# A graph layer with linear attention and an expert FFN: gates from features not yet normed, the list of other slots behind the first gathers, a slot's result by halves in one step, and its last rows gathered sooner

## The chip, the cores and the metric

The kernel runs on one core of a Trainium2 chip. The metric is the device time of one execution in microseconds (us), as the median of several runs. A core has five engines with an instruction stream each: TensorE (PE, matrix products; its weight loads are shown apart as PEld), VectorE (DVE), ScalarE (ACT), GpSimd (POOL) and SyncE (SP). In this kernel SP issues the ordinary DMAs, and POOL issues the indirect ones, which gather or scatter rows by a list of row numbers. Matrix results land in PSUM, a memory of eight banks; everything else is in SBUF, 128 partitions wide.

## The reference

There are 1250 nodes with 768 features. Three sublayers follow one another; the first two add to the same input.

```python
xn = layernorm(x)
x  = x + gnn(xn) + mix(xn)          # gnn: two graph attention layers, then concat([xn, out2]) @ Wu + bu
x  = x + ffn(layernorm(x))          # mix: linear attention with 12 heads, then @ Wo + bo

def ffn(xt):                        # 8 experts, 768 -> 384 -> 768
    gate = xt @ Wg + bg
    scores, idx = top_k(gate, 2)
    h = gelu(einsum('td,edh->eth', xt, W1) + b1)
    y = einsum('eth,ehd->etd', h, W2) + b2
    comb = sum(one_hot(idx, 8) * scores[..., None], axis=1)
    return einsum('te,etd->td', comb, y)
```

`layernorm` has no gain and no bias: it takes off the mean of a row and divides by its standard deviation. `out2` is the output of the second graph layer, 2 heads of 96 features. The gate's scores are used as they are, without a softmax. Everything is float32.

## The kernel before, in words

*Stages.* Up to about 620 us the kernel norms x and computes the two graph attention layers and the sums of the linear attention. What the graph layers leave is `o2T`, the second layer's output per head, turned, and `rd2`, one over its softmax sums. Then two stages follow that the change touches.

*The pair stage* (some 620 to 885 us). The nodes are 10 tiles of 125 rows, taken as 5 pairs. The loop `for p in range(NT // 2)` computes for both tiles of a pair x + mix + gnn. It first loads the two tiles of x (`xt`, L932) and adds the biases `bu_b` to them (L933). Then it calls `query(p + 1)`, the query products of the next pair, and then makes the present pair's products with `Wu` and `Wo`. The products with `Wq` and `Wu` are by quarters: a pair of tiles is a 2 x 2 array of blocks, and seven products of sums and differences of blocks replace eight. Each is a sequence of matmuls into one PSUM bank (`product`, L801), which VectorE then adds into the query or into xt (`add`, L945). `s_p` is the pool of 4 such banks, and `mm_p` the pool for turning and for other products. After the even tile's last product comes `finish(2 * p, ...)`, after the odd tile's `finish(2 * p + 1, ...)`.

*finish(t, xt)* (L853 to L922) does the rest for one tile, in this order. Four products of `o2T` with the last rows of Wu (L860) are the graph part; VectorE scales each by `rd2` and adds it to xt (L862). xt goes to the output (L865). `normalise` (L300 to L311) makes the normed row `xl` from it: statistics (L307, L308), standard deviation on ACT (L309), reciprocal (L310), result (L311). xl goes to `xl_d` in DRAM (L870). `turn` (L314 to L321) transposes xl by six TensorE transposes, three to a bank, and ACT copies each bank (L321). Six matmuls with `Wg` give the gates (L875, two records each), VectorE adds the bias (L878), and the 8 gates are written to `xl_d` beside the row (L880). VectorE ranks the 8 gates of each node (L887 to L896); `sel` marks its two experts. A product with a triangle of ones and one with `ones` and the running count `cum` (L900) give each node's place within its experts; adding `base` (L903) makes it a place in the whole list. An expert has NJ = 10 slots of 128 rows. The place is cut into slot and row within the slot by integer steps (L909 to L914), both become one-hot matrices (`hot` L918, `put` L920), and their product (L922) adds node numbers into `inv`, the PSUM tile of row lists, 128 rows by 80 slots.

*Between the stages* (L977 to L1012). After the last tile VectorE turns `inv` into `idx`, the row lists in SBUF (empty places point to a spare row). SP issues the loads of experts 1 to 3 (`expert`, L692 to L700: W1, W2 and the bias `wb` spread over the partitions). Then VectorE works out the list of other slots: the first FIX = 3 slots of each expert are always computed, the others only where nodes fill them. That is a chain of small VectorE operations on tiles of 8 to 64 elements, with three small TensorE steps, which ends in `v_row` and `e_row` (number and expert of the other slots in order) and `n_more` (how many there are). Here there is one.

*The expert stage* (some 903 us to the end). For each expert, `gather` (L1021) fetches its three slots: POOL issues an indirect DMA of 128 rows of 776 numbers (L1027), TensorE turns them by six transposes into `px` (L1030), VectorE copies px in two halves (L1033) into `xsT` and copies the gate column (L1036). px is one PSUM buffer of two banks (`x_p`, bufs 1). `inner` (L1039) makes `ph` = W1 times xsT for 384 rows (L1046) and ACT makes gelu of it, `hT` (L1048). The next expert's gather is called here, ahead of `give`. `give` (L1051) makes `py` for each slot (L1058), VectorE adds the bias row `wb` to all 768 columns in one step (L1061), ACT multiplies by the gate (L1062), and POOL issues an indirect DMA that adds the rows `ys` into the output (L1063). Two buffers each serve py and ys. Then the weights of expert e + 4 are called for (four weight buffers). After the loop `other(0)` does the same for the first other slot: it reads its number and expert into registers (L1082, L1084), copies its rows and bias, loads its expert, gathers, computes and scatters. `others(1)` does the rest under an If, and has nothing to do here.

*What sets the order.* The program is written as one sequence, and the framework spreads it over the engines. Each engine runs its own instructions in a fixed order in which priorities decide and which isn't wholly that of the text; between engines semaphores make an instruction wait for its inputs, and for the last use of a buffer that it overwrites. An instruction that waits holds up all behind it on its engine. DMAs share 8 semaphores in turn, so an SP or POOL instruction may also wait for an earlier DMA on the same semaphore.

## Time and profile before

| | |
|---|---|
| median of 3 runs | 1147.31 us (1145.44 to 1149.77) |
| the profiled execution, its own time | 1146.65 us |
| its span, first to last instruction | 1144.8 us |
| mean granted TensorE clock | 0.976 |
| PE, PEld | 1046.8, 700.9 us busy (91%, 61%) |
| DVE, ACT, POOL | 705.8, 347.9, 74.2 us busy (62%, 30%, 6%) |
| DMA | 79.76 MB, mean 70 GB/s |

Busy time by stretch of the profiled execution:

| stretch, us | PE | DVE | ACT | POOL | granted clock |
|---|---|---|---|---|---|
| 0 to 400 | 350.83 | 304.50 | 158.83 | 7.23 | 0.99 |
| 400 to 620 | 205.65 | 165.91 | 109.21 | 2.97 | 0.98 |
| 620 to 885 (pairs) | 264.32 | 171.96 | 39.02 | 0.00 | 1.00 |
| 885 to 915 (between) | 12.94 | 14.69 | 1.14 | 5.51 | 0.61 |
| 915 to 1112 (experts) | 197.00 | 44.91 | 35.78 | 52.28 | 0.99 |
| 1112 to 1145 (end) | 16.09 | 3.80 | 3.91 | 6.21 | 0.79 |

How to read such rows: a row of the timeline begins with the start and the busy length in us, then engine, line of the code, operation, output and inputs by the program's names, shapes, and how many instructions are joined in the row; in brackets stand the idle time before it and what ended it. A group of instructions on PE that overlap is given by its whole length. The clock is the share of full speed that TensorE was granted. The span leaves out what lies before the first and after the last instruction; the execution's own time has it.

### The profile page before, as it was taken

The numbers are of one execution on the slowest core, as the hardware profiler recorded it, in microseconds if no ns is written. First come the engines' busy times: TensorE is split into PE (matmuls) and PEld (weight loads), VectorE is DVE, ScalarE is ACT, GpSimd is POOL, SyncE is SP. The second block draws the span as 40 slices with busy tenths as digits, with TensorE's granted clock in tenths as the row PEclk, the third lists the DMA queues.
The fourth block names the chain that finished last, engine by engine and source line by source line (L and its number), as shares of the span: only waits on it lengthen the run. The fifth ranks groups of instructions, "written<-read, shape, count | busy, mean of one in ns | idle before, by whom it ended". The sixth has DMA issues, their size and how long they took to land.

```text
span 1144.8 us, 12035 instructions
## 1 busy us (share of the span) xinstructions
PE 1046.8 (91%) x4482; PEld 700.9 (61%) x4482; DVE 705.8 (62%) x1439; ACT 347.9 (30%) x522; POOL 74.2 (6%) x98
## 2 busy tenths in 40 slices
PE   2699998999999989988999999999999499999994
PEld 2596655579696969544554556666665256666653
DVE  7866767569696967769685857566665422222210
ACT  2141114464655555174743211120200011111121
POOL 1000000000000000000000000000000212223221
PEclk9999999999999999989999999999999599999997
DMA  5015000000000000200035011112045638787543
GB/s 161 28 31 189 14 28 1 1 1 1 1 1 1 1 1 3 80 1 1 14 129 169 12 41 41 47 36 63 20 158 180 197 72 220 208 215 189 118 63 50
DMA packets 35542, 79.76 MB, mean 70 GB/s; under 512 B 7006, under 2 KB 15536, under 8 KB 35468
## 3 DMA queue, kind: packets, MB, share of 16 engines
q1 hardware_dynamic: 29868, 59.06, 16.0%
q0 software_dynamic: 5600, 19.77, 8.6%
q8 instruction: 39, 0.64, 0.2%
q14 instruction: 35, 0.29, 0.1%
HBM read 60.48 MB, written 18.34 MB: 69 GB/s over the span
## 4 chain that ended last, share of the span: by engine, by line
PE 67%; DVE 23%; DMA 3%; issue 2%; ACT 2%; SPq 0%; POOL 0%; DVEq 0%; POOLq 0%; ACTq 0%
PE s L801 16%; PE ph L1046 9%; PE mm L599 8%; PE py L1058 7%; PE mm L430 7%; DVE scr L520 6%; DVE w L540 5%; DVE w L541 5%; PE ag L553 3%; PE mm L860 2%; PE ag L575 2%; PE mm L405 2%; PE px L1030 2%; PE ec L350 1%; PE g L875 1%
## 5 line engine op out<-in xcount | busy, mean ns | idle before, releaser
L553 PE MATMUL ag<-kept,w 125*125 125x198 f32 x800 | 137.5, 333 | 5.1 <-DVE w L541 4.8
L553 PEld LDWEIGHTS ag<-kept,w 125*125 125x125 f32 x800 | 133.5, 188 | 9.0 <-DVE w L541 9.0
L1046 PE MATMUL ph<-xsT,w 128*128 128x384 f32 (+1 forms) x324 | 102.3, 478 | 2.7 <-DVE xsT L1033 2.7
L1058 PE MATMUL py<-w,hT 128*128 128x384 f32 x300 | 100.6, 486 | 0.0
L430 PE MATMUL mm<-Wg,xnT 128*125 128x400 f32 x240 | 90.1, 513 | 1.1 <-DVE xnT L321 0.6
L540 DVE TENSOR_TENSOR w<-v,w 125x1250 f32<-125x1250 f32 x60 | 86.4, 1456 | 6.6 <-ACT w L538 5.9
L599 PE MATMUL mm<-Wv_sb,xnT 128*125 128x384 f32 x240 | 85.8, 490 | 4.8 <-DVE kvacc L619 4.8
L520 DVE CUSTOM_DVE_ANT_0 scr<-ss_row,mask 125x1250 bf16<-125x1250 f32 x60 | 87.4, 1456 | 0.5 <-ACT ss_row L511 0.2
L1046 PEld LDWEIGHTS ph<-xsT,w 128*128 128x128 f32 x324 | 61.5, 201 | 42.2 <-DVE xsT L1033 3.4
L541 DVE SCALAR_TENSOR_TENSOR w<-w,AT 125x1250 f32<-125x1250 f32 x60 | 86.5, 1457 | 0.4
L539 ACT ACTIVATE v<-dn_row,sl 125x1250 f32<-125x1250 f32 x60 | 79.3, 1333 | 17.0 <-DVE w L540 16.5
L599 PE MATMUL mm<-Wk_sb,xnT 128*125 128x384 f32 x240 | 84.5, 486 | 0.0
L801 PE MATMUL s<-w,qT 128*125 128x384 f32 x240 | 83.7, 491 | 0.0
L1033 DVE COPY xsT<-px 128x384 f32<-128x384 f32 x50 | 25.5, 552 | 87.3 <-PE px L1030 87.3
L1058 PEld LDWEIGHTS py<-w,hT 128*128 128x128 f32 x300 | 55.4, 190 | 33.8
L1061 DVE TENSOR_TENSOR ys<-py,wb 128x768 f32<-128x768 f32 x25 | 23.9, 958 | 74.1 <-PE py L1058 50.8
L599 PEld LDWEIGHTS mm<-Wv_sb,xnT 128*125 128x125 f32 x240 | 42.5, 187 | 31.1 <-DVE kvacc L619 6.9
L801 PEld LDWEIGHTS s<-w,qT 128*125 128x125 f32 x240 | 43.3, 188 | 26.9 <-issue 0.2
L538 ACT ACTIVATE w<-up_row,s 125x1250 f32<-125x1250 f32 x40 | 53.3, 1331 | 17.8 <-PE ag L553 17.6
L430 PEld LDWEIGHTS mm<-Wg,xnT 128*125 128x125 f32 x240 | 42.6, 190 | 26.1 <-ACT v L367 1.3
L599 PEld LDWEIGHTS mm<-Wk_sb,xnT 128*125 128x125 f32 x240 | 42.2, 187 | 23.5 <-issue 1.7
L356 DVE TENSOR_TENSOR AT<-AT,ec 125x120 f32 x162 | 44.4, 274 | 19.8 <-PE ec L350 18.6
(296 smaller groups left out, 1466.9 us busy)
## 6 DMA issues: line engine op xcount, KB each, us to landing
w<-in_L_ffn_W_dram SPq DMA_DIRECT2D x18, 1152.0 KB
xt<-in_x_dram SPq DMA_DIRECT2D x20, 336.0 KB
wb<-in_L_ffn_b_dram SPq DMA_DIRECT2D x9, 384.0 KB
out_dram<-xt SPq DMA_DIRECT2D x10, 336.0 KB
xl_d<-xl SPq DMA_DIRECT2D x10, 336.0 KB
W_sb<-in_L_gnn_W_dram SPq DMA_DIRECT2D x1, 2304.0 KB
Wk_sb<-in_L_mix_Wk_dram SPq DMA_DIRECT2D x1, 2304.0 KB
Wv_sb<-in_L_mix_Wv_dram SPq DMA_DIRECT2D x1, 2304.0 KB
```

The source lines that it names most:

```text
L356: nc.vector.tensor_add(here, here, ec[:, g])
L430: nc.tensor.matmul(ps[:PT, :2 * (CG + 2)], xnT[:, c, t * PT:(t + 1) * PT], Wg1[:, c, 2 * k:2 * k + 2].rearrange("p h c -> p (h c)"), start ...
L520: nc.vector.tensor_tensor_reduce(scr, ss_row, mask[:, t], 1.0, 0.0, ALU.mult, ALU.max, top[:, t:t + 1])
L538: nc.scalar.activation(w, up_row, AF.Exp, bias=ss[:, st:st + 1])
L539: nc.scalar.activation(v, dn_row, AF.Exp, bias=sl[:, st:st + 1])
L540: nc.vector.tensor_tensor(w, v, w, op=ALU.max)
L541: nc.vector.scalar_tensor_tensor(w, w, 2.0, AT[:, st, :N], op0=ALU.min, op1=ALU.mult)
L553: nc.tensor.matmul(ag[:, t // 2, o:o + CG], w[:, t * PT:(t + 1) * PT], gw[:, st, hd], start=st == 0 and t % 2 == 0, stop=st == NT - 1, ski ...
L599: nc.tensor.matmul(ps[:PT, :384], xnT[:, c, t * PT:(t + 1) * PT], w[:, c, half], start=c == 0, stop=c == KC - 1)
L801: nc.tensor.matmul(ps, left[:, c], right[:, c], start=start and c == 0, stop=c == n - 1, skip_group_check=True)
L1046: nc.tensor.matmul(ph[:, :n * 128], w[0][:, o:o + 128], xT[:, c, :n * 128], start=c == 0, stop=c == KC - 1)
L1058: nc.tensor.matmul(py[:, k, :384], hT[:, f, j * 128:(j + 1) * 128], w[:, o:o + 384], start=f == 0, stop=f == FC - 1)
```

## The change

The tile's graph part is taken out of `finish` into `second(t, xt)`, which the pair loop calls for each tile as soon as its x and biases are in xt, ahead of `query(p + 1)`. In `finish` the transposes and the gate product take xt, not the normed xl. Since xl = (xt - mean) / sd, the gates follow as (xt Wg - mean times the column sums of Wg) / sd + bg: `Wg_s`, the column sums, is made once by a product of ones with Wg, and VectorE needs `nrs` (minus one over sd), `off` and the gate step in place of one addition. The part `base` of a node's place comes from a third product into pp, so the addition `at` goes; `slot_row` counts in steps of 128, so the slot needs no shift: `row_f` is the place's last seven bits, `slot_f` the rest.

Between the stages, only `total` is still computed ahead of the gathers. The rest of the list stands behind the first `gather`, with its constants in the longer-lived pool `fp`, and its transposes go into the pool of ph.

`gather` issues all its DMAs ahead of the transposes, and px is now a half with a bank of its own (`x_p`, bufs 2). In `give`, py is a half of 384 columns in one bank (`y_p`, bufs 4); ACT multiplies the bias row by the gate ahead of it (`gb`), and VectorE makes ys from PSUM in one step per half, py times gate plus gb. The other slot's register loads, rows, bias and weights (`other`) come at the end of the loop's step e = 4, where the ring has no more to load, and its gather comes with the call for expert 7, ahead of expert 7's py products; the rest of it (`run`) stays behind the loop.

The line numbers after the change, where they differ: products L813, graph part L872 and L874, gates L891, `off` L896, gate L898, places L920, `row_f` L932, `slot_f` L933, hot and put L937 and L939, inv L941, xt's load and biases L951 and L952, `total` L997 and L999, `idx` L1001 and L1002, gather L1018, px L1027, xsT L1028, gates' column L1031, ph L1041, hT L1043, gb L1050, py L1057, ys L1059, scatter L1061, register loads L1069 and L1071, list L1096 to L1120.

The diff, cut to its core:

```diff
+        Wg_s = rp.tile([PT, NE], F32)
+        all1 = rp.tile([128, PT], F32)
+        nc.gpsimd.memset(all1, 1.0)
+        pf = g_p.tile([128, 2 * NV], F32, name="g")
+        for c in range(KC):
+            nc.tensor.matmul(pf[:PT, :NE], all1, Wg_sb[:, c], start=c == 0, stop=c == KC - 1)
+        nc.scalar.copy(Wg_s, pf[:PT, :NE])
...
-        def finish(t, xt):
+        def second(t, xt):
             tk = tokens(t)
             for h in range(H2):
...
                     nc.vector.scalar_tensor_tensor(xt[:, half], ps[:PT, :384], rd2[:, h, t:t + 1],
                                                    xt[:, half], op0=ALU.mult, op1=ALU.add)
+
+        def finish(t, xt):
...
-            normalise(xl[:, :D], xt)
+            mv, rs = normalise(xl[:, :D], xt)
+            nrs = rl.tile([PT, 1], F32, name="nrs")
+            nc.vector.tensor_scalar(nrs, rs, -1.0, None, op0=ALU.mult)
...
-            turn(xT, xl, mm_p, "mm", nc.scalar.copy)
+            turn(xT, xt, mm_p, "mm", nc.scalar.copy)
...
-            nc.vector.tensor_add(gate, pg[:PT, :NE], bg_b)
+            nc.vector.scalar_tensor_tensor(off, Wg_s, mv[:, 0:1], pg[:PT, :NE], op0=ALU.mult,
+                                           op1=ALU.subtract)
+            nc.vector.scalar_tensor_tensor(gate, off, nrs, bg_b, op0=ALU.mult, op1=ALU.add)
...
-            for i, (l, r) in enumerate(((tri, sel), (ones, cum[:, t]))):
+            for i, (l, r) in enumerate(((ones, base), (ones, cum[:, t]), (tri, sel))):
...
-            at = rl.tile([PT, NE], F32, name="at")
-            nc.vector.tensor_add(at, pp[:PT, :NE], base)
...
-            nc.vector.tensor_single_scalar(s_i[:, 0], b_i, 7, op=ALU.arith_shift_right)
-            nc.vector.tensor_single_scalar(s_i[:, 1], b_i, 127, op=ALU.bitwise_and)
-            s_f = rl.tile([PT, 2, 2], F32, name="s_f")
-            nc.vector.tensor_copy(s_f, s_i)
+            nc.vector.tensor_single_scalar(r_i, b_i, 127, op=ALU.bitwise_and)
+            nc.vector.tensor_copy(row_f, r_i)
+            nc.vector.tensor_sub(slot_f, both, row_f)
...
                 nc.vector.tensor_add(xt, xt, bu_b)
+                second(t, xt)
                 x2.append(xt)
...
+        pt = g_p.tile([128, 2 * NV], F32, name="g")
+        nc.tensor.matmul(pt[:, :NE], ones, cum[:, NT], start=True, stop=True)
+        total = fp.tile([128, NE], F32)
+        nc.vector.tensor_copy(total, pt[:, :NE])
         free = rp.tile([128, NV], F32)
...
-        more = rp.tile([128, NE, NJ - FIX], F32)
...
-            nc.vector.tensor_scalar(row, pr[:1, :128], add, None, op0=ALU.add)
...
-    x_p = ctx.enter_context(tc.tile_pool(name="x_p", bufs=1, space=PSUM))
+    x_p = ctx.enter_context(tc.tile_pool(name="x_p", bufs=2, space=PSUM))
...
-    y_p = ctx.enter_context(tc.tile_pool(name="y_p", bufs=2, space=PSUM))
+    y_p = ctx.enter_context(tc.tile_pool(name="y_p", bufs=4, space=PSUM))
...
+        got = []
+        for r in rows:
+            xg = sp.tile([128, D + NE], F32, name="xg", bufs=3)
+            nc.gpsimd.indirect_dma_start(xg, None, xl_d, bass.IndirectOffsetOnAxis(r, 0))
+            got.append(xg)
...
+        for j, xg in enumerate(got):
             for a in range(2):
+                px = x_p.tile([128, 512], F32, name="px")
+                for c in range(3):
+                    o = (3 * a + c) * 128
+                    nc.tensor.transpose(px[:, c * 128:(c + 1) * 128], xg[:, o:o + 128], ident)
                 nc.vector.tensor_copy(xT[:, 3 * a:3 * a + 3, j * 128:(j + 1) * 128],
-                                      px[:, a, :384].rearrange("p (b n) -> p b n", b=3))
+                                      px[:, :384].rearrange("p (b n) -> p b n", b=3))
...
+        gb = sp.tile([128, D], F32, name="gb")
+        nc.scalar.mul(gb, wb, gates)
+        ys = sp.tile([128, D], F32, name="ys")
+        for k in range(2):
+            half = slice(k * 384, (k + 1) * 384)
+            py = y_p.tile([128, 512], F32, name="py")
+            for f in range(FC):
                 o = KC * FF + f * D + k * 384
...
-        nc.vector.tensor_add(halves(ys), py[:, :, :384], halves(wb))
-        nc.scalar.mul(ys, ys, gates)
+            nc.vector.scalar_tensor_tensor(ys[:, half], py[:, :384], gates, gb[:, half],
+                                           op0=ALU.mult, op1=ALU.add)
...
-        xT, gates = gather([rows], ee)
+        return ee, rows, bias, w
+
+    def run(rows, bias, w, got):
+        xT, gates = got
         hT = inner(w, xT, 1, bias)
         give(w, hT, 0, rows, gates[:, :1])
...
-    other(0)
+    ahead = gather(fixed(0), 0)
+
+    more = fp.tile([128, NE, NJ - FIX], F32)
...
+        nc.vector.tensor_scalar(row, pr[:1, :128], add, None, op0=ALU.add)
+
+    for e in range(NE):
...
+            ahead = gather(fixed(e + 1), e + 1)
+        else:
+            ahead = gather([first[1]], first[0])
         for j, rows in enumerate(fixed(e)):
             give(ring[e], hT, j, rows, gates[:, j:j + 1])
         if e + 4 < NE:
             ring.append(expert(fW1[e + 4], fW2[e + 4], fb2[e + 4]))
+        elif e + 4 == NE:
+            first = other(0)
+    run(*first[1:], ahead)
     others(1)
```

## The prediction

> **What bounds the kernel now.** I read the page first (shares and the chain that ended last), then the engines' busy time by stretch, then the timeline around the two places where TensorE is not full.
>
> ```profile
> span 1144.8 us, 12035 instructions
> ...
> PE 1046.8 (91%) x4482; PEld 700.9 (61%) x4482; DVE 705.8 (62%) x1439; ACT 347.9 (30%) x522; POOL 74.2 (6%) x98
> ...
> PE 67%; DVE 23%; DMA 3%; issue 2%; ACT 2%; SPq 0%; POOL 0%; DVEq 0%; POOLq 0%; ACTq 0%
> ```
>
> ```profile
> 660.00:714.00 54.00, 54.00 (x204) 32.86 (x203) 35.10 (x95) 8.66 (x15) 0.00 (x0) 1.00 0.14 43
> 884.00:898.00 14.00, 8.05 (x35) 5.08 (x33) 7.94 (x29) 1.14 (x3) 0.00 (x0) 0.78 0.55 189
> 898.00:907.00 9.00, 1.20 (x4) 0.37 (x4) 3.90 (x28) 0.00 (x0) 3.09 (x3) 0.50 0.89 308
> 915.00:919.00 4.00, 4.00 (x7) 2.16 (x8) 0.57 (x3) 0.00 (x0) 0.43 (x1) 0.50 0.34 101
> 943.00:968.00 25.00, 25.00 (x90) 15.16 (x89) 6.11 (x12) 4.54 (x6) 7.69 (x6) 1.00 0.79 206
> ```
>
> The columns are length, then busy us (and count) of PE, PEld, DVE, ACT, POOL, then granted clock, DMA share, GB/s. A pair of node tiles takes 54 us of full TensorE, an expert 25.3 us, also full. So work on other engines there is free, and work on PE costs its own length. The hole is 885 to 915 (clock down to 0.50), and a second lies at the end. The timeline of the hole:
>
> ```profile
> 884.98 3.15 PE L860 MATMUL mm<-Wu_sb,kept 96*125 96x384 f32 x8
> 887.51 1.26 DVE L862 SCALAR_TENSOR_TENSOR xt<-mm,rd,xt 125x384 f32<-125x384 f32 x2 [0.36 <-PE mm L860]
> 890.52 0.68 DVE L311 TENSOR_SCALAR xl<-xt,ln_mv,ln_rs 125x768 f32<-125x768 f32 x1
> 892.41 2.69 PE L875 MATMUL g<-Wg_sb,xT 128*125 128x8 f32 x12 [0.20 <-ACT xT L321]
> 895.13 0.17 DVE L878 TENSOR_TENSOR xl<-g,bg_b 125x8 f32<-125x8 f32 x1 [3.94 <-PE g L875]
> 900.25 0.23 DVE L978 SCALAR_TENSOR_TENSOR idx<-inv,free 128x80 int32<-128x80 f32 x1
> 902.24 0.28 DVE L1012 TENSOR_SCALAR e_row<-g 1x128 int32<-1x128 f32 x1 [0.47 <-PE g L1011]
> 903.20 1.17 POOL L1027 DMA_INDIRECT xg<-xl_d,idx  x1 [293.92 <-PE g L1011]
> 907.34 1.52 PE L1030 MATMUL px<-ident,xg 128*128 128x128 f32 x6 [5.13 <-DMA xg<-xl_d,idx]
> 910.01 1.51 PE L1030 MATMUL px<-ident,xg 128*128 128x128 f32 x6 [1.16 <-DVE gates L1036]
> 914.85 14.01 PE L1046 MATMUL ph<-xsT,w 128*128 128x384 f32 x36 [0.65 <-DVE xsT L1033]
> ```
>
> Everything here is one chain: last product, graph part (L862), norm, transposes, gates, ranking, idx, list of other slots, gather, px, ph. And the end:
>
> ```profile
> 1112.20 1.55 POOL L1063 DMA_INDIRECT out_dram<-ys,idx  x1 [7.78 <-ACT ys L1062]
> 1118.93 0.96 DVE L1061 TENSOR_TENSOR ys<-py,wb 128x768 f32<-128x768 f32 x1 [4.15 <-DMA out_dram<-ys,idx]
> 1119.56 1.55 POOL L1063 DMA_INDIRECT out_dram<-ys,idx  x1 [5.80 <-DMA out_dram<-ys,idx]
> 1120.40 5.91 PE L1046 MATMUL ph<-xsT,w 128*128 128x128 f32 x36 [2.10 <-DVE xsT L1033]
> 1132.48 1.55 POOL L1063 DMA_INDIRECT out_dram<-ys,rows  x1 [5.31 <-ACTq L1098]
> ```
>
> Here VectorE stands at ys until the first scatter lands, the px copies behind it are late, and so is the last ph.
>
> **The change, part by part.** Let P be when PE has issued its last product of tile 9: 884.9 before.
>
> *Tile 9, P to idx.* Before, the gate add starts at 895.13 = P+10.2. After, the graph part is already in xt, so from the built order: add to xt (0.56) ends P+0.8; the first half's transposes stand ahead of it, the second half's (0.32) follow; two copies on ACT (0.42 each) end P+1.85; the last three gate matmuls end P+2.5. They take 1.21 for all twelve records as at 694.2, not 2.69: PE no longer idles 3.1 us first, so the clock has not dropped. VectorE: off P+2.7, reciprocal, xl (0.68, it stands ahead of the gate), nrs, gate at P+4.0. Gain 6.2. The base add (`at`, 0.2) leaves the chain; the row and slot steps keep four dependent casts, even. idx ends P+9.2 against P+15.6: **-6.4**.
>
> *List behind the gathers.* Before, the gather starts 2.7 us after idx (903.20 against 900.48). After, its VectorE wait is the idx write; with POOL's issue row (0.86 after the last release) that is 0.9. **-1.8**. The list still runs on VectorE ahead of the first gates copy: from idx 2.0 to e_row and 1.4 to the rows copy, inside the 4.1 us that the gather takes to land. If that cover went, each us costs one. SP is moved too: expert 3's load is issued some 4.6 us before the gather instead of 7.0, so the gather shares the queues longer: **+0.4** (0 to 2). xl's first row DMA now waits for expert 2's first load on a shared semaphore; that was issued near P-9.5 and such a pair needs 8, so it is hidden.
>
> *px by halves in two banks.* Before, gather to ph is 11.65, px in steps of 2.67 because one buffer waits for both copies. After: landings at 4.1, about 5.6 and 7.1; each half takes 0.76 at the low clock and its copy 0.55; VectorE's order puts the second and third gates copies (which wait for their gathers) between. ph at about 9.05. **-2.6**.
>
> *Clock.* ph needs 11.61 at full clock (942.56 to 954.17) and took 14.01, since 4.3 us of dense work ran at 0.50. [...] I take the middle, **-1.2**.
>
> *PE work moved ahead of P.* Tile 9's four graph products: **+2.6** (4 x 0.65); the other nine tiles' were already inside the full stretch. On VectorE their 4 x 0.6 lie under PE.
>
> *New PE work.* Wg_s, six matmuls of 8 columns: 1.2 by the gate row, part of it in PE's waits near 640: **+1.0** (0.3 to 2). The base product per tile: the pair L900 costs 0.06 and makes the next product 0.75 instead of 0.65; a second interruption is 0.15 (0.05 to 0.25), nine times before P: **+1.35**.
>
> *New waits in the pair stage.* Transposes and gates come in halves with one product (0.65) between, and the copy from transposes to gates needs 0.75: 0.1, ten times. VectorE's four graph adds per tile stand ahead of the adds that free PE's banks. I followed it from X, the end of the odd tile's xt: the last query add before the fourth product ends X+19.3, PE gets there X+19.4; the ranking's sel is ready X+9.25, PE wants it X+9.3. Nothing spare: **+1.2** (0 to 4).
>
> *give.* One step from PSUM by halves (0.55 each, as L1033/L862) in place of 0.96 + 0.94; gb on ACT runs two results ahead. In the experts PE is full, so nothing, as long as bank and ys are free; ys still waits for a scatter, but under the next ph (11.6). PE's count per expert is the same.
>
> *End.* With Z = ph of expert 7 done (1106.04): px stands ahead of py, so ph and py of the other slot end Z+22.1, its scatter could go Z+23.15. But scatters go one by one: first at Z+5.65 (before Z+6.16), then 7.36, 6.06 and 5.9 as the rows have it: Z+25.0 against 26.44: **-1.4**. [...]
>
> Sum: -6.4 -1.8 +0.4 -2.6 -1.2 +2.6 +1.0 +1.35 +1.2 -1.4 = **-6.85**. The profiled execution took 1146.65 (span 1144.8 and 1.85 around it): 1139.8; the median of the runs is 0.66 higher, so **1140**. 0.5%, about what a measurement of this kernel can tell from no change, is 5.7 us.
>
> **Rivals.**
> *A, cheaper still:* the new PE work falls into PE's waits (-2.3), the pair stage has no stalls (-1.2), ph is warm (-1.2): 1135. For it: PE has waits between 618 and 645. Against: at 660 to 884 it has none.
> *B, the pair stage eats it:* stalls at the upper bound (+2.8), gather late (+1.6), ph cold (+1.2): 1145.6. For it: nothing spare on VectorE.
> *C, slower:* the odd tile's x load comes late. It is issued after the gates' write (X+5.5), lands near X+9, and VectorE's add stands in order at X+12.15 ahead of all that frees PE's banks. Later than that, every us stops PE in each of four pairs. At X+13.9 the gain is gone, at X+15.3 it is 0.5% slower: 1153. Against: loads of this size landed 2.9 to 3.3 us after issue.
> *D, the gather waits anyway* (a pool's release in place of the list): -1.8 lost, 1142.
>
> **How the numbers follow.** Forecast 0.50 (own range 1137 to 1143), A 0.14, B 0.14, C 0.16, D 0.06. Faster by over 0.5% is below 1141.6: 0.42 of the forecast's 0.50, all of A, 0.03 of B and D: 0.59. Slower: C, 0.16. Within: 0.25. The range 1132 to 1150 takes in the bounds of A, B and D and leaves out most of C and a little below.
>
> **What would show it.** Right: tile 9's gate about 4 us after its last product, gate matmuls at 1.2; the gather within 1 us of idx; px without 1.1 us waits and ph about 9 after the gather; PE full in the pair stage, 1 to 1.5 us longer per pair at most; ph under 13; last scatter 25 after ph of expert 7. Wrong: PE waits on VectorE or an xt load in 640 to 885, a pair of over 56 us, an expert of over 25.5, or a gather that lands after 6.

## The result, and the profile after

The changed kernel takes 1138.52 us (median of 6 runs, 1137.44 to 1141.00) against 1148.05 us for the kernel before (median of 6 runs, 1145.44 to 1150.60): a ratio of 0.9918, with an interval from 0.9900 to 0.9936. That is 9.4 us by the ratio. The forecast was 1140, its own range 1137 to 1143. The profiled execution of the changed kernel took 1141.00 us, which is the longest of the six, and its span is 1139.0 us, 5.8 below that of before. The page:

```profile
span 1139.0 us, 12140 instructions
...
PE 1046.9 (92%) x4504; PEld 700.1 (61%) x4504; DVE 716.0 (63%) x1474; ACT 348.4 (31%) x523; POOL 76.2 (7%) x101
...
PE 68%; DVE 22%; DMA 5%; issue 2%; ACT 2%; POOL 1%; SPq 0%; DVEq 0%; POOLq 0%; ACTq 0%
```

TensorE is busy for the same 1047 us; its idle time is 5.9 us shorter. The timeline of the changed kernel between the stages, from tile 9's last product to the first ph (start, length, then engine, line and what was done):

```profile
892.30 1.52 PE L813 MATMUL s<-w,qT 128*125 128x384 f32 x4
893.86 0.55 DVE L965 TENSOR_TENSOR xt<-xt,s 125x384 f32<-125x384 f32 x1 [2.13 <-PE s L813]
894.84 1.55 PE L891 MATMUL g<-Wg_sb,xT 128*125 128x8 f32 x12
897.53 0.23 DVE L898 SCALAR_TENSOR_TENSOR xl<-off,nrs,bg_b 125x8 f32<-125x8 f32 x1
902.56 0.22 DVE L1002 SCALAR_TENSOR_TENSOR idx<-inv,free 128x80 int32<-128x80 f32 x1
903.85 1.17 POOL L1018 DMA_INDIRECT xg<-xl_d,idx  x1 [290.73 <-DVE one L1117]
904.28 0.28 DVE L1120 TENSOR_SCALAR e_row<-ph 1x128 int32<-1x128 f32 x1
908.69 4.65 PE L1027 MATMUL px<-ident,xg 128*128 128x128 f32 x18 [4.44 <-DMA xg<-xl_d,idx]
913.34 12.60 PE L1041 MATMUL ph<-xsT,w 128*128 128x384 f32 x36
```

The gate's step starts 3.7 us after the last product ends (893.82), the gather starts 1.07 us behind idx and ahead of the end of the list (e_row), px is one unbroken group of 18, and ph starts 4.65 us after the first of them. The end of the changed kernel:

```profile
1107.98 1.55 POOL L1061 DMA_INDIRECT out_dram<-ys,idx  x1 [7.08 <-DVE ys L1059]
1114.28 1.55 POOL L1061 DMA_INDIRECT out_dram<-ys,idx  x1 [4.75 <-DVE ys L1059]
1114.62 4.18 PE L1041 MATMUL ph<-xsT,w 128*128 128x128 f32 x36
1120.65 1.55 POOL L1061 DMA_INDIRECT out_dram<-ys,idx  x1 [4.82 <-DMA out_dram<-ys,idx]
1127.27 1.55 POOL L1061 DMA_INDIRECT out_dram<-ys,rows  x1 [5.06 <-DMA out_dram<-ys,idx]
```

The last scatter waits for the one ahead of it, as the sum assumed, and starts 24.75 us behind the end of expert 7's ph (1102.52). In the stretches, with the same columns as before, a pair and an expert are still full; the clock is low, at 0.50, from 897.8 to 914.8 us:

```profile
660.00:714.00 54.00, 54.00 (x206) 32.56 (x205) 34.85 (x95) 8.35 (x15) 0.00 (x0) 1.00 0.15 44
897.80:911.43 13.63, 4.10 (x18) 2.57 (x17) 7.70 (x45) 2.07 (x3) 4.01 (x4) 0.50 0.81 289
911.43:914.80 3.37, 3.35 (x11) 1.86 (x10) 2.19 (x6) 1.09 (x1) 1.91 (x3) 0.50 0.66 157
943.00:968.00 25.00, 25.00 (x91) 15.39 (x90) 6.91 (x15) 4.54 (x6) 7.72 (x6) 1.00 0.79 202
```

I cut both profiled executions at the same events (starts of records, us) and take the differences. "Pair stage" is from the start of the first product by quarters to the start of tile 9's last one.

| stretch | before | after | difference | predicted |
|---|---|---|---|---|
| up to the pair stage (no part of the change) | 593.82 | 596.00 | +2.2 | 0 |
| pair stage | 290.79 | 297.34 | +6.55 | +6.15 |
| to the end of idx | 15.87 | 9.44 | -6.4 | -6.4 |
| idx to the first gather | 2.71 | 1.08 | -1.6 | -1.8 |
| gather to the first px | 4.14 | 4.83 | +0.7 | +0.4 |
| first px to ph | 7.52 | 4.66 | -2.9 | -2.6 |
| the first ph | 14.01 | 12.60 | -1.4 | -1.2 |
| to the end of expert 7's ph | 177.18 | 176.57 | -0.6 | 0 |
| to the last scatter, and from there to the end | 38.71 | 36.52 | -2.2 | -1.4 |

The sum is -5.7, the span's difference within rounding. Without the first row, in which the change has no part, it is -7.9 against the predicted -6.85.

### The profile page after: what moved, and what is told of

Same layout as the page of the kernel before. It is cut to its first block, busy times and chain, and to the rows that moved or that the text cites. A ratio compares the mean times of both kernels' runs of the same rounds, so it can differ in the third digit from the quotient of the medians.

```text
span 1139.0 us, 12140 instructions
## 1 busy us (share of the span) xinstructions
PE 1046.9 (92%) x4504; PEld 700.1 (61%) x4504; DVE 716.0 (63%) x1474; ACT 348.4 (31%) x523; POOL 76.2 (7%) x101
## 4 chain that ended last, share of the span: by engine, by line
PE 68%; DVE 22%; DMA 5%; issue 2%; ACT 2%; POOL 1%; SPq 0%; DVEq 0%; POOLq 0%; ACTq 0%
PE s L813 17%; PE ph L1041 8%; PE mm L599 8%; PE mm L430 7%; PE py L1057 7%; DVE scr L520 6%; DVE w L540 5%; DVE w L541 5%; PE ag L553 3%; PE mm L872 2%; PE ag L575 2%; PE mm L405 2%; PE px L1027 2%; DMA out_dram<-ys,idx 1%; PE ec L350 1%
## 5 line engine op out<-in xcount | busy, mean ns | idle before, releaser
L1057 PE MATMUL py<-w,hT 128*128 128x384 f32 x300 | 100.6, 486 | 0.0
L1041 PE MATMUL ph<-xsT,w 128*128 128x384 f32 (+1 forms) x324 | 99.2, 466 | 0.0
L1041 PEld LDWEIGHTS ph<-xsT,w 128*128 128x128 f32 x324 | 59.3, 192 | 38.8 <-issue 0.6
L813 PE MATMUL s<-w,qT 128*125 128x384 f32 x240 | 82.7, 492 | 0.0
L1028 DVE COPY xsT<-px 128x384 f32<-128x384 f32 x50 | 25.8, 553 | 82.7 <-PE px L1027 82.6
L1057 PEld LDWEIGHTS py<-w,hT 128*128 128x128 f32 x300 | 55.3, 190 | 33.6
L1059 DVE SCALAR_TENSOR_TENSOR ys<-py,gates,gb 128x384 f32<-128x384 f32 x50 | 30.2, 616 | 69.6 <-PE py L1057 40.1
L813 PEld LDWEIGHTS s<-w,qT 128*125 128x125 f32 x240 | 43.2, 188 | 28.0 <-issue 1.8
L1050 ACT ACTIVATE gb<-wb,gates 128x768 f32<-128x768 f32 x25 | 23.4, 935 | 112.7 <-DVE ys L1059 99.0
```

What stands on the lines that cost most here:

```text
L813: nc.tensor.matmul(ps, left[:, c], right[:, c], start=start and c == 0, stop=c == n - 1, skip_group_check=True)
L1041: nc.tensor.matmul(ph[:, :n * 128], w[0][:, o:o + 128], xT[:, c, :n * 128], start=c == 0, stop=c == KC - 1)
L1057: nc.tensor.matmul(py[:, :384], hT[:, f, j * 128:(j + 1) * 128], w[:, o:o + 384], start=f == 0, stop=f == FC - 1)
```

## Experiments

Each starts from the changed kernel and undoes or adds one thing; one starts from the kernel before. They ran on three chips, each beside runs of the kernel before, so ratios compare them better than medians do. Single runs of one kernel differ by up to 9 us (of the kernel before, by 12), so most single parts show only in the stretches of the profile; those are what I judge by, one profile to an experiment. A repeat of the same code gives the size of their noise: in seven profiles whose pair stage is the same (the changed kernel, and the experiments list_in_rp, result_two_steps, other_last, kept_busy, scatter_plain, list_first) it took 295.97 to 297.34 us, with 296.48 in the middle, and in the two with the old code 290.79 and 290.66. So the pair stage grew by 5.8, and the changed kernel's own profile lies 0.9 above the middle. The spread sits in two groups: the products of `Wo` with the sums of the linear attention (L681; 9.40 to 10.98 us from one record's start to the next) and the products by quarters; all the rest of the stage is the same in the seven within 0.05 us. The time of the last scatter varies too: over the eight profiles with the changed kernel's end and px by halves it comes at 24.06 to 25.07.

| label | median us | ratio to before (interval) | pair stage | to idx | to gather | px to ph | first ph | last scatter |
|---|---|---|---|---|---|---|---|---|
| changed kernel | 1138.52 | 0.9918 (0.9900 to 0.9936) | 297.34 | 9.44 | 1.08 | 4.66 | 12.60 | 24.75 |
| normed_gates | 1140.48 | 0.9937 (0.9912 to 0.9962) | 294.49 | 12.35 | 1.08 | 5.08 | 12.58 | 25.07 |
| graph_part_late | 1138.60 | 0.9925 (0.9905 to 0.9945) | 292.76 | 12.50 | 1.07 | 4.66 | 12.70 | 24.58 |
| list_in_rp | 1139.94 | 0.9928 (0.9912 to 0.9945) | 296.25 | 9.44 | 2.90 | 5.06 | 12.33 | 24.32 |
| px_whole | 1144.64 | 0.9969 (0.9955 to 0.9983) | 302.34 | 9.45 | 1.07 | 7.54 | 14.72 | 24.60 |
| result_two_steps | 1139.01 | 0.9922 (0.9899 to 0.9944) | 295.97 | 9.45 | 1.08 | 4.66 | 11.88 | 25.70 |
| other_last | 1138.75 | 0.9927 (0.9910 to 0.9943) | 296.49 | 9.46 | 1.08 | 4.42 | 11.88 | 24.44 |
| base_added | 1137.80 | 0.9915 (0.9894 to 0.9935) | 296.20 | 9.68 | 1.08 | 4.64 | 11.88 | 24.21 |
| kept_busy | 1144.51 | 0.9986 (0.9971 to 1.0002) | 296.32 | 9.45 | 1.08 | 5.58 | 12.73 | 24.06 |
| halves_alone | 1142.86 | 0.9954 (0.9934 to 0.9975) | 290.66 | 16.23 | 2.71 | 4.59 | 11.88 | 25.36 |
| last_tile_only | 1138.09 | 0.9917 (0.9889 to 0.9945) | 294.19 | 9.45 | 1.07 | 4.66 | 12.45 | 24.30 |
| scatter_plain | 1134.20 | 0.9887 (0.9847 to 0.9927) | 296.63 | 9.45 | 1.06 | 4.66 | 12.69 | 21.09 |
| list_first | 1138.81 | 0.9926 (0.9902 to 0.9951) | 296.48 | 9.45 | 1.07 | 4.33 | 11.88 | 24.34 |

"Last scatter" is counted from the end of expert 7's ph.

### px in one buffer again

```diff
+            px = x_p.tile([128, 2, 512], F32, name="px")     # x_p: bufs 1
+            for c in range(KC):
+                nc.tensor.transpose(px[:, c // 3, ...], xg[:, c * 128:(c + 1) * 128], ident)
             for a in range(2):
-                px = x_p.tile([128, 512], F32, name="px")    # x_p: bufs 2
...
```

> The changed kernel with the transposes of a gathered slot into one buffer of two banks again, free only when both copies are done. Forecast: first gather to ph 11.65 us in place of 9.5 (+2.15), that ph colder or equal (12.6 to 13.6); the seven later experts up to +0.1 each, since before they took 177.2 us together and now 176.6. Total +2.5 against the changed kernel, 1141. Rival (the landings of the second and third gather, 1.5 us apart, set the pace and not the buffer): +0.5 or less, 1138.8.

The timeline of this kernel:

```profile
912.67 1.54 PE L1025 MATMUL px<-ident,xg 128*128 128x128 f32 x6 [4.88 <-DMA xg<-xl_d,idx]
915.37 1.51 PE L1025 MATMUL px<-ident,xg 128*128 128x128 f32 x6 [1.16 <-issue]
918.04 1.51 PE L1025 MATMUL px<-ident,xg 128*128 128x128 f32 x6 [1.16 <-issue]
920.21 14.72 PE L1041 MATMUL ph<-xsT,w 128*128 128x384 f32 x36 [0.65 <-DVE xsT L1028]
```

The pace of 2.7 us a slot and the waits of 1.16 us are back, so the buffer sets it and not the landings: the rival falls. But the loss is 6 us by the medians where 2.5 was expected. Px to ph has +2.9, the first ph +2.1 (the clock comes back only within it, after 5.8 us), and the seven later experts +0.6 (177.19 against 176.57, and 177.18 before the change); these make 5.6. This one profile also has a stretch at half clock in the pair stage, where the code is that of the changed kernel, and which makes its 302.34:

```profile
622.00:636.00 14.00, 14.00 (x32) 7.72 (x31) 4.35 (x6) 0.67 (x4) 0.00 (x0) 0.51 0.31 110
```

It is left out of the account; the 6 us are those of the median of 10 runs.

### The kernel before with px by halves alone

The edit is the reverse of the one above, made in the kernel before: px of 512 columns inside `for a in range(2)`, `x_p` with two buffers, and nothing else.

> The kernel before with one part of the change alone: px by halves in two buffers of one bank. Theory (the px buffer was worth 6 us of the change's 9.4, twice what the prediction gave it): first px to ph 4.7 to 5.1 us in place of 7.52, the first ph 11.9 to 12.6 us in place of 14.0 since denser transposes bring the clock back sooner, the seven later experts 176.6 us in place of 177.2; total -4.6 to -5.3 against the kernel before, a ratio of about 0.9955. Rival (only with the other parts, the earlier gathers and the result in one step, do the halves run through): px to ph above 6 us, ph at 14, total -2 or less.

```profile
905.02 1.51 PE L1032 MATMUL px<-ident,xg 128*128 128x128 f32 x6 [5.14 <-DMA xg<-xl_d,idx]
906.88 2.71 PE L1032 MATMUL px<-ident,xg 128*128 128x128 f32 x12 [0.35 <-DMA xg<-xl_d,idx]
909.61 11.88 PE L1046 MATMUL ph<-xsT,w 128*128 128x384 f32 x36
```

Measured: px to ph 4.59, ph 11.88, the later experts 176.58, and a ratio of 0.9954 where 0.9955 was expected. The halves need none of the other parts. By the ratio they are 5.3 us of the change's 9.4 (its interval, 0.9934 to 0.9975, allows 2.9 to 7.6), by the stretches 5.7: half or a little more, from one edit of a few lines. The profile is that of the shortest of the ten runs (1137.10; the longest took 1145.56), so its stretches count here and not its total.

### The norm and the graph part, each put back

```diff
-            turn(xT, xt, mm_p, "mm", nc.scalar.copy)
+            turn(xT, xl, mm_p, "mm", nc.scalar.copy)
...
-            nc.vector.scalar_tensor_tensor(off, Wg_s, mv[:, 0:1], pg[:PT, :NE], op0=ALU.mult, op1=ALU.subtract)
-            nc.vector.scalar_tensor_tensor(gate, off, nrs, bg_b, op0=ALU.mult, op1=ALU.add)
+            nc.vector.tensor_add(gate, pg[:PT, :NE], bg_b)
```

> The changed kernel with the transposes and the gate product taken from the normed row again (no column sums of Wg, one addition as the gate's step); the graph part stays early. Forecast of the theory (gates from unnormed features take the norm out of tile 9's chain): from tile 9's last product to idx 12.1 us in place of 9.0 (+3.1: statistics, deviation, reciprocal and the normed row, 2.4 together, stand ahead of the transposes, which before took 0.95 and two copies, 0.84); the first ph +0.7 us as TensorE idles longer; the pair stage -1.23 (no column sums) and up to -0.8 (TensorE's gate products no longer wait for a copy that is late by 0.08 us ten times). Total about +1.8 against the changed kernel, 1140. Rival (the norm was hidden behind something else that ends as late, so this part of the change only cost its work): idx at 9 us as it is, total -2, 1136.5.

```profile
892.59 0.68 DVE L311 TENSOR_SCALAR xl<-xt,ln_mv,ln_rs 125x768 f32<-125x768 f32 x1
893.42 1.13 PE L319 MATMUL mm<-ident,xl 125*128 125x125 f32 x6 [2.83 <-DVE xl L311]
```

The transposes (L319) wait for the normed row again. Idx comes 12.35 us after the last product in place of 9.44 (+2.9, expected +3.1), and the pair stage is 294.49, 2.0 below the middle of the seven. So this part gives about 1 us net by the stretches, where +1.8 was expected and the medians have 2.0, which their intervals can't hold apart. The colder first ph that was forecast did not come here or in the next experiment (12.58 and 12.70 against 12.60). The rival with idx at 9 falls.

```diff
         def finish(t, xt):
+            second(t, xt)
...
                 nc.vector.tensor_add(xt, xt, bu_b)
-                second(t, xt)
```

> The changed kernel with the four graph products and their four additions back at the head of the work that follows a tile's last product; gates from unnormed features stay. Forecast (the graph part only moved, TensorE pays its 2.9 us ahead of tile 9's last product instead of behind it): pair stage to tile 9's last product -2.9 us, from there to idx +3.2 (before, the last product's addition to the end of the graph part took 3.07 us), the first ph +0.7 by a colder clock: +1.0 us, 1139.5. Rival 1 (the early graph part makes VectorE late, which costs TensorE waits in every pair): the pair stage gains over 4.5 us, total -1 or less, 1137.5. Rival 2 (a large part of the measured gain is this one): over +3 us, 1141.5 or more.

```profile
887.99 3.08 PE L872 MATMUL mm<-Wu_sb,kept 96*125 96x384 f32 x8
890.46 1.26 DVE L874 SCALAR_TENSOR_TENSOR xt<-mm,rd,xt 125x384 f32<-125x384 f32 x2 [0.36 <-PE mm L872]
```

These rows stand behind tile 9's last product again, and idx comes 3.06 us later (forecast 3.2); the pair stage is 3.7 shorter than the middle (forecast 2.9, rival 1 over 4.5). From the pair stage's begin to the first ph this version comes to 316.10 and the changed kernel, with the middle of the seven for its pair stage, to 316.5; the medians are 1138.60 and 1138.52, the ratios 0.9925 and 0.9918. The graph part's move is worth nothing that shows. It moves 3 us from the hole into the pair stage; the 0.8 above its 2.9 is no more than that stage's spread.

### The two parts for the last tile alone

```diff
-                second(t, xt)
+                if t == NT - 1:
+                    second(t, xt)
...
+            last = t == NT - 1
+            if not last:
+                second(t, xt)
...
-            turn(xT, xt, mm_p, "mm", nc.scalar.copy)
+            turn(xT, xt if last else xl, mm_p, "mm", nc.scalar.copy)
```

The gate's step follows `last` in the same way, and `Wg_s` is computed ahead of the graph layer's bias product.

> The changed kernel with the graph part early, and the gates from unnormed features, for the last tile alone; the other nine tiles as before the change; the column sums of Wg moved to a place where TensorE waits 2 us anyway, ahead of the graph layer's bias product near 620 us. Theory (the two parts cost 3.3 and 1.9 us in the pair stage, of which the last tile's four products, 2.6, and a small rest are needed): from the bias product to tile 9's last product 267.3 to 268.2 us in place of 270.9, from there to the first ph 20.0 as it is, total -2.7 to -3.4, 1135.4. Rival (the order that the other tiles get costs waits, as the kernel before had spare time only because its last tile came later): 270 or more, total within 1 us of the changed kernel.

Idx at 9.45 as in the changed kernel, and a pair stage of 294.19, 2.3 below the middle where 2.7 to 3.4 was expected. (The expectation counts from the bias product, from where this profile has 268.79, and the changed kernel and its repeats 270.9 to 271.5.) The rival, 270 or more, falls. The median, 1138.09, is that of the changed kernel within the interval: a gain of 2 us is read from the stretches of one profile and not shown by the times.

### The list: its place, and its memory

```diff
-        total = fp.tile([128, NE], F32)
+        total = rp.tile([128, NE], F32)      # and so on for more, slots, cover, end, ..., one
...
-    ahead = gather(fixed(0), 0)              # the list stands ahead of it, in the closed pool rp
```

> The changed kernel with the list of other slots written ahead of the first gathers again, its tiles in the pool that is closed there, its two small transposes in the bank of the gates. The instructions come out in the same order on every engine; what is different is that the first gather's buffer lies in the closed pool's memory, so that it waits for TensorE's last read of the list (the wait for PE ends later than idx). Forecast: idx to gather 2.7 us in place of 1.07, gather to landing 4.2 to 4.8, total +1.2 to +1.7 against the changed kernel, 1140. Rival (the gather waits for something else as long, as in rival D of the prediction): no change, 1138.5.

```profile
902.19 0.22 DVE L1002 SCALAR_TENSOR_TENSOR idx<-inv,free 128x80 int32<-128x80 f32 x1
904.36 0.28 DVE L1032 TENSOR_SCALAR e_row<-g 1x128 int32<-1x128 f32 x1 [0.46 <-PE g L1031]
905.31 1.17 POOL L1046 DMA_INDIRECT xg<-xl_d,idx  x1 [291.46 <-SPq L1099]
```

The gather starts 2.90 us behind idx, behind the end of the list. The second experiment writes the list ahead of the gathers too, but keeps its tiles in the pool that stays open:

```diff
+        more = fp.tile([128, NE, NJ - FIX], F32)   # the whole list, ahead of the first gather
...
     ahead = gather(fixed(0), 0)
-    more = fp.tile([128, NE, NJ - FIX], F32)
```

> The changed kernel with the list of other slots written ahead of the first gathers, its tiles kept in the pool that stays open; its two transposes in the bank of the gates. Forecast (the place in the text does nothing, the pool does): idx to gather 1.07 us as in the changed kernel, total 0. Rival (the place in the text does it): 2.7 to 2.9 us, total +1.4.

```profile
900.52 0.22 DVE L1002 SCALAR_TENSOR_TENSOR idx<-inv,free 128x80 int32<-128x80 f32 x1
901.81 1.17 POOL L1046 DMA_INDIRECT xg<-xl_d,idx  x1 [289.88 <-DVE one L1029]
902.69 0.28 DVE L1032 TENSOR_SCALAR e_row<-g 1x128 int32<-1x128 f32 x1 [0.47 <-PE g L1031]
```

Here it is 1.07 us, and the gather starts ahead of the end of the list. The two experiments differ only in the pool of the list's tiles and constants, so the place in the text does nothing and the pool does it. That the first gather's buffer takes over the closed pool's memory is read from the code (the pool `sp` is opened where `rp` is closed), not from a trace. Of the 1.8 us the landing gives some back: gather to first px takes 4.19 in list_in_rp and 4.83 in the changed kernel.

### The result in two steps, and the other slot last

```diff
-            nc.vector.scalar_tensor_tensor(ys[:, half], py[:, :384], gates, gb[:, half], op0=ALU.mult, op1=ALU.add)
+        nc.vector.tensor_add(halves(ys), py[:, :, :384], halves(wb))
+        nc.scalar.mul(ys, ys, gates)
```

> The changed kernel with a slot's result in two steps again: VectorE adds the bias row to all 768 columns behind the last py matmul, ACT multiplies by the gate behind it; py again in two buffers of two banks. Forecast (in the experts TensorE is full, so only the end feels it): the experts' 176.6 us between the first and the last ph stay within 0.3; first scatter behind the last ph at 6.2 us in place of 5.46, the last at 25.5 in place of 24.75, since the scatters follow one another at 6.2 to 6.6 us; total +0.7, 1139.2. Rival (the new form is what keeps VectorE's px copies on time): TensorE waits for px or bank in the experts, 1 us or more each at some experts, total +3 or more.

```profile
1108.11 1.55 POOL L1058 DMA_INDIRECT out_dram<-ys,idx  x1 [8.28 <-ACT ys L1057]
1126.99 1.55 POOL L1058 DMA_INDIRECT out_dram<-ys,rows  x1 [5.08 <-DMA out_dram<-ys,idx]
```

The experts take 176.58 us as expected. The first scatter starts 6.82 us behind expert 7's ph (5.46; forecast 6.2), the last 25.70 (24.75): +0.95 where 0.75 was expected, and outside the 24.06 to 25.07 of the eight profiles. The rival falls.

```diff
-        else:
-            ahead = gather([first[1]], first[0])
...
+    first = other(0)
+    run(*first[1:], gather([first[1]], first[0]))
```

> The changed kernel with the other slot's register loads, rows, bias, weights and gather behind the loop again. Forecast (the last scatter then waits for its own result and not for the scatter ahead of it): px of the other slot behind the last py, ph some 2 us later and at the lower clock, last scatter 25.4 to 26 us behind the last ph in place of 24.75; total +0.6 to +1.3, 1139.5. Rival (the chain of scatters binds alone and hides the late gather): the last scatter at 24.75 as it is, 1138.5.

```profile
1105.25 1.55 POOL L1061 DMA_INDIRECT out_dram<-ys,idx  x1 [6.67 <-DVE ys L1059]
...
1117.29 1.55 POOL L1061 DMA_INDIRECT out_dram<-ys,idx  x1 [4.57 <-DMA out_dram<-ys,idx]
...
1124.89 1.55 POOL L1061 DMA_INDIRECT out_dram<-ys,rows  x1 [6.05 <-DVEq L1088]
```

Here the forecast failed. The last scatter comes 24.44 us behind expert 7's ph, within the spread of the changed kernel's end: its row ends a wait for something else than the scatter ahead, as expected, and it is 7.6 us behind that in place of 6.6, but the first scatter goes 0.66 us sooner (4.80), since no px stands ahead of expert 7's py (six transposes take 0.65 us on TensorE). Gathering the last rows sooner is worth nothing that shows here.

### Scatters that overwrite

```diff
         nc.gpsimd.indirect_dma_start(out, bass.IndirectOffsetOnAxis(rows, 0), ys, None,
-                                     compute_op=ALU.add)
+                                     )
```

> The changed kernel with scatters that overwrite the output rows in place of adding to them (the sum over two experts and the residual is left out of the output). Forecast (the 6.2 to 6.6 us from one scatter to the next are the order kept between scatters into one output, with the fetch for adding as a part): 4 to 5 us from one to the next at the end, the last scatter 20.9 to 22 us behind the last ph in place of 24.75, bound by its own result; total -3. Rival (the time of a scatter is that of issue and landing whatever it does): 6.2 us as it is, total 0.

```profile
1107.07 0.97 POOL L1061 DMA_INDIRECT out_dram<-ys,idx  x1 [14.21 <-DVE ys L1059]
1110.94 0.97 POOL L1061 DMA_INDIRECT out_dram<-ys,idx  x1 [2.90 <-DVE ys L1059]
1114.80 0.97 POOL L1061 DMA_INDIRECT out_dram<-ys,idx  x1 [2.90 <-DVE ys L1059]
1122.69 0.97 POOL L1061 DMA_INDIRECT out_dram<-ys,rows  x1 [6.92 <-DVE ys L1059]
```

Each scatter now waits for its own result alone, the first three 3.87 us from one to the next, and the last goes at 21.09, 3.7 us sooner. The total is 4.3 us below the changed kernel by the medians (two runs; the intervals overlap). So the end is bound by adding scatters that go one by one, some 6.3 us each. The profile's median from issue to landing is 6.6 us for the adding scatters and 3.8 for those that overwrite, so most of the difference is in the landing itself; how much of that is the adding and how much the order between scatters isn't split further.

### The base product

```diff
-            for i, (l, r) in enumerate(((ones, base), (ones, cum[:, t]), (tri, sel))):
+            for i, (l, r) in enumerate(((tri, sel), (ones, cum[:, t]))):
...
+            nc.vector.tensor_add(at, pp[:PT, :NE], base)
```

> The changed kernel with base added by VectorE again in place of the third product. Forecast of the prediction's step (the products of base cost 1.35 us in the pair stage): pair stage 296.0 us in place of 297.3, tile 9's idx +0.2 later; total -1.1, 1137.4. Rival (records of the changed kernel: TensorE starts its next product 0.03 us after the base product, 0.76 us for all of L920 against 0.47): pair stage -0.3, total -0.1, 1138.4.

The pair stage is 296.20 against 296.48 in the middle, idx 0.23 later: the rival is right, and the prediction's 1.35 us wrong. (The 0.3 is within the stage's spread, but 1.35 would have brought 295.1, below all seven.) The changed kernel's timeline shows why: the base product comes with that of cum, and the next product starts 0.03 us behind.

```profile
886.09 0.17 PE L920 MATMUL g<-base,ones 125*128 125x8 f16 x1
886.12 0.17 PE L920 MATMUL g<-cum,ones 125*128 125x8 f16 x1
886.15 2.83 PE L813 MATMUL s<-w,qT 128*125 128x384 f32 x8
```

### TensorE kept busy

```diff
+                if t == NT - 1 and i == 2:
+                    fill(ident, xT[:, 3:5], 4)             # ahead of the ranking's product
+            if t == NT - 1:
+                fill(ident[:PT], xl[:, :2 * PT], 2)
...
+            for i in range(28):                            # behind the first gathers' issue
+                nc.tensor.matmul(ps[:, :NV], ident, free, start=i == 0, stop=i == 27)
```

> The changed kernel with idle matmuls on TensorE between tile 9's gates and the first gather's landing (6 of 250 columns ahead of the ranking's product, 28 of 80 columns behind the last one-hot product; what they compute is not used). Theory (the lower clock between 897.8 and 914.8 us comes from TensorE's idle stretches, and costs time in the small products, the px transposes and ph): the clock stays at 1.00 or dips for one stretch of 3.4 us, the first ph takes 11.7 us in place of 12.6, first px to ph 4.3 in place of 4.66, total -1.3 to -1.7, 1137. Rival 1 (such small matmuls are not counted as work by what sets the clock): clock as it is, total 0. Rival 2 (they delay the ranking or px): idx or px later by 0.5 or more, total above 0.

```profile
895.70:899.10 3.40, 1.30 (x7) 0.74 (x6) 3.08 (x22) 0.00 (x0) 0.00 (x0) 1.00 0.75 183
899.10:912.00 12.90, 12.41 (x58) 12.16 (x58) 1.73 (x14) 0.00 (x0) 3.09 (x3) 0.50 0.66 255
```

Both rivals hold. TensorE still idled while VectorE ranked (1.30 us busy of 3.40), and the clock fell to 0.50 at 899.1; then the matmuls of 80 columns filled 12 us without bringing it back. They took 12.24 us in place of some 6 (an estimate: 56 records at the 0.107 us that a transpose takes in the full-clock pair stage), and px had to wait: it starts 11.1 us after the gather in place of 4.8. The ratio is 0.9986, no gain over the kernel before. Whether wider matmuls would hold the clock wasn't tried.

## Why the prediction was right, point by point

**Tile 9, P to idx (-6.4).** Right, -6.43. The norm's part is 2.9 of it and the graph part's 3.1, by the two experiments that put them back.

**PE work moved, new PE work, new waits (+2.6, +1.0, +1.35, +1.2).** The sum of 6.15 was close to the 6.55 of the profile and the 5.8 of the middle, but one of its terms was wrong. From one TensorE record's start to the next, added up by kind over the stage in the two profiles: the graph products +2.9, the column sums 1.23, the gate products +0.3 beside them, the one-hot products +0.7, the place products +0.3, the products by quarters +1.1. The last is not the change's: in halves_alone, whose pair stage is that of before, the products by quarters take 219.03 us against 217.81 before and 218.88 in the changed kernel, and L681 gives the difference back (9.57 against 10.90 before). The two groups together are 228.7 and 228.6 in the profiles with the old pair stage and 229.0 in the middle of the seven, so the change adds 0.3 to them. The step that failed is thus the base product (1.35; its removal gave 0.3). The new waits, 0.3 and 0.7 and 0.3, are about the 1.2 of the forecast, and the graph products and column sums a little over theirs, which hid part of the miss. The larger gaps stand at the gate and one-hot products, in pieces of about 0.1 us, too short for the view of waits; what each piece waits for was not followed. Rival C did not come: from 640 us to the last product that view of the changed kernel (total, times, longest, in us) has one line,

```profile
PE s L813 <- DVE qy L833: 0.3, 1, 0.3
```

The part of the change up to idx therefore gains 6.4 us behind the last product and pays 5.8 to 6.55 ahead of it. Its gain alone would not be measurable.

**List behind the gathers (-1.8 + 0.4).** Right in size, -1.6 and +0.7, and rival D fell. The reason given was not the one: it was the pool of the list's tiles and not the list's place, as list_first shows. The number came right because the same edit also moved the tiles. What makes the landing later (the loads that share the queues, by the forecast) was not tested.

**px by halves (-2.6) and the clock (-1.2).** Right in kind. The px step was -2.9. The clock's -1.2, the middle of 0 and the 2.4 between 14.01 and 11.61, was the author's guess, and no run ahead of the result shows it; with the halves ph takes 11.88 to 12.73 us, so the term is -1.3 to -2.1 and goes with where px starts in a stretch of low clock (below). Left out was the 0.6 us that the halves save in the later experts. Together 5.3 to 6 by the two experiments against 3.8 predicted: of the gains it is the most mis-sized, enough to account for the difference between 1140 and 1138.5.

**give in the experts (0).** Right: 176.58 with the old form too.

**End (-1.4).** The chain of scatters bound, as the sum had it (before, a scatter landed 5.3 to 10.5 us after its issue, 5.7 in the middle), and the last scatter came at 24.75 where 25.0 was predicted. That the numbers meet is in part luck: the sum took the spacings as 7.36, 6.06 and 5.9, and they came as 6.30, 6.37 and 6.62. And the early gather gives nothing that shows (other_last), the form of the result 0.95. Before, the spacings were 7.35, 6.07 and 6.86 us. The kernel before with nothing changed at the end but px by halves has 6.26, 6.39 and 6.55, and its last scatter at 25.36, so about 1 us of the -2.2 in the table is not from the new end. Why the spacings were longer in that one profile of before stays open.

**Rival A** needed a pair stage without waits, **rival B** stalls at their bound: neither came, though a ph near that of A (11.88 against 11.61 at full clock) did in five experiments.

Measured one at a time, the parts come to about the whole: px by halves 5.3 to 6 us, the list's pool 1.2, the norm about 1, the form of the result 0.95, the graph part's move, the early gather and the base product nothing that shows. That is some 8.5 to 9 of the 9.4, each from one profile or from medians that vary as said.

## What to carry to other kernels

Work that was moved from an idle stretch into a full one was paid at about its whole length there (the graph part: idx 3.06 us sooner, the pair stage 2.9 to 3.7 longer): weigh the two stretches against each other, and move only the piece that is late (here the last tile's, by the stretches 2 us better). A buffer that had to be free as a whole between two engines cost more than its own waits of 1.16 us a slot, since the clock also stayed low for longer in the work behind it (px_whole: px to ph +2.9 us, the first ph +2.1). When a wait stands ahead of a transfer, look whose memory its buffer takes over before moving lines of code (the first gather came 2.90 us behind idx with the list in the closed pool, and 1.07 or 1.08 with it in the open one, in either place in the text).

## What was not expected of the hardware

**The transposes brought the clock back where they filled a whole stretch of 3.41 us.** Between the stages the clock stands at 0.50 for multiples of 3.41 us in these traces (13.65, 17.1, 20.5, 23.9, 27.3; it is 27.3 in the kernel before and 17.1 in the changed kernel). In the changed kernel such a stretch begins 0.7 us before the first px; the clock comes back at the end of the next one, 1.5 us into ph, and ph takes 12.60 us. In result_two_steps px starts at 908.17 and the stretch from 908.7 on is full of it:

```profile
908.76:912.17 3.41, 3.38 (x16) 2.32 (x15) 2.48 (x7) 0.00 (x0) 1.58 (x2) 0.51 0.39 106
912.17:924.70 12.53, 12.23 (x42) 7.18 (x41) 1.49 (x5) 2.44 (x3) 1.28 (x2) 1.00 0.26 87
```

ph starts at full clock and takes 11.88. In all five profiles with 11.88 (result_two_steps, other_last, base_added, halves_alone, list_first), px starts before a stretch or at most 0.18 us into it; in the six others with px by halves and no idle matmuls (the changed kernel, normed_gates, graph_part_late, list_in_rp, last_tile_only, scatter_plain), 0.29 to 0.98 us into it, with ph at 12.33 to 12.70. So in these eleven profiles ph started at full clock where px by halves had filled a stretch, and not where it began later; what sets the length and the start of the stretches is not shown. Not every matmul had that effect: in kept_busy those of 80 columns filled more than two such stretches without a gap (12.24 us), and the clock stayed at 0.50; its px was idle for 0.98 us within the next stretch, and the clock came back one stretch later (an estimate from its ph: 12.73 us is 0.85 over 11.88, so 1.7 us of it were at half clock, up to 919.6 us). No version here set the start of px within a stretch on purpose.

**The part ahead of the change.** The pair stage starts at 594.3 to 597.8 us in the 12 profiles that have the rest of the change, and at 593.8 and 591.3 in the two without it, while the change touches nothing ahead of it but a few small constants. The later starts go with stretches of low clock between 160 and 200 us (at 0.50, the changed kernel has 3.4 us from 163.9 and 6.8 from 191.2, the kernel before 3.4 from 192.2). Two profiles of the one kind are too few to say if the change shifts those stretches, or chance does; the 2.2 us of the table's first row are such a slip.
